# Score products of a retention layer issued in turn over four row groups, with a third group of batches in the scans' PSUM banks and a new set of planner figures

## The chip, the cores and the metric

The program runs on one core of a Trainium2 chip. The metric is the device time of one execution in microseconds; a kernel's time is the median over its runs. A trace exists of one execution, whose own time is given beside its span (from the first instruction to the last).

Names of the engines: PE is the matrix engine (TensorE; PEld is its weight loads), DVE is VectorE, ACT is ScalarE, POOL is GpSimd, SP is the engine that only issues transfers here. PEclk is the share of full speed that PE's clock was granted.

## The reference, cut to what matters

Two layers work on x of shape (16, 256, 128), that is 16 batches of 256 positions. Each layer is an attention-like part and an expert part, both with a modulated layer norm ahead and a gated residual behind. All is float32.

1. **Layer 0, retention.** Eight heads of 16 features keep a state that decays from position to position. The kernel computes it by products:

```python
S = g * S + k_t[..., :, None] * v_t[..., None, :]
y_t = jnp.einsum('bhde,bhd->bhe', S, q_t)
```

   Behind it come a group norm over the positions and a projection.

2. **Layer 0, experts.** Each of 8 experts chooses its 64 best positions of every batch (`top_k` over positions), with an exact Gelu between two products.
3. **Layer 1, selective scan.** For 256 inner features and 16 states each, with a short convolution and gates around it:

```python
dA = jnp.exp(dt_t[..., None] * A)
h = dA * h + dt_t[..., None] * b_t[:, None, :] * u_t[..., None]
y = jnp.einsum('bdn,bn->bd', h, c_t)
```

4. **Layer 1, experts.** Each position goes to its best 2 of 8 experts, with a gated product of width 448.

## The kernel before, in words

**A planner writes the order.** The function `adaln_two_layers` states the work as *chains*: a chain is a list of operations of which each follows the one before it, with an urgency (`pl.chain(urgency)`). A chain may need the end of other chains' steps (`need`, `done`) or a free buffer (`take`, `give`). `Plan.issue` then goes through all chains while the program is built. It keeps a clock for each engine, takes the operation that can start first (among those within 0.15 us on that engine, the one of the smallest urgency), and so fixes the order of every engine's instructions. Durations come from the table `USUAL` (by engine, name of the output and its length) or, where it has no entry, from the `us=` of the call. The urgencies are in `U`: `A` is that of the four groups of retention, `E` of the layer-0 experts with `Eh` and `Eo` for their two products, `front` of what prepares a batch for the scans, and `exp`, `dB`, `scan`, `sum` of the scans' parts. On the chip every engine then runs its list in order and waits where an operand is missing. In the trace nearly every operation has line 174, that of the planner's call, so rows are told apart by tiles.

**Retention** (`retention(g)`, groups of four batches, g = 0 to 3). For a batch b, `scores(b)` norms x, transposes it (pta, hTa), makes q and k together (pqk), copies q, and makes two masked copies of k, ke and ko, with the even and the odd heads (DVE and ACT). Then pv and v, pk, kd and the state S. The score products follow: for each j of four, the 32 features 32j to 32j+31 (two heads) of ke and ko are multiplied with q for both halves of the positions, four products of 32 rows x 128 x 128 into a bank of PSUM that is j's own. DVE multiplies the bank with the decay table and writes pr (`pr{b}_{j}`, 128 x 512). `outputs0(b)` multiplies pr with v into four groups of 32 columns (py) and takes statistics (yst). `group_norm`, `project` and `expert_scores` follow for a group, and `choose` selects the positions, in a series of small DVE operations (m, wk, sp).

**The banks.** The tuple `own` says where the score products go. The names va, vg, vx, vy are tokens for the four banks which the scans use later (two for dA, one for h, one for the sums ya). The token e stands for two banks of the common pool `ps_w`, shared with other work. `EARLY` is the number of groups that use the scans' banks; `recur`, which adds the scans' chains to the plan, waits for their last score products and for the first group's Gelus.

**Layer-0 experts** (`experts_of(q)`, four batches at a time): gather by products (gg, px, xin), first product (ph), Gelu (hg), second product (pye, ysb), and the way back by products (gt, pos, fres).

**Scans** (`scans`, 256 units: 16 batches of 16 units, a unit having 128 partitions and two scans of 256 positions side by side). `front(b)` makes bt, u and dd for a batch, with pb, pxs and pdt on PE; spl on ACT uses a logarithm. For each unit ACT makes dA by two exponentials into one of two PSUM buffers, POOL makes dB (twelve buffers), DVE runs the scan h, multiplies h with ct into dB, and PE sums (ya). The exponential, the logarithm and the exact Gelu need different function tables on ACT; the build adds a table load wherever the next function isn't in the table at hand. The planner isn't told of these loads but by durations: `us=1.88` for a Gelu of the last three expert groups (0.6 for the first) and 3.2 for the logarithm.

**Layer-1 experts** (`expert(g, j)`, 92 tiles of 128 positions; px, pa, pg, sl, pm, py at line 1576, yt) start while the scans run; 47 tiles come behind the last scan.

Of the kernel before, what the change touches and what calls it, by code (L numbers as in the profile page):

```python
# [11 lines left out]
F32 = mybir.dt.float32  # L12
# [3 lines left out]
ALU = mybir.AluOpType  # L16
# [3 lines left out]
P = 128  # L20
B, L, D = 16, 256, 128
NCH = L // P
H0, DH = 8, 16
E, CAP, HF = 8, 64, 512
# [3 lines left out]
T = 2 * L  # L28
# [1 line left out]

GROUPS = ((0, 1), (2, 3), (4, 5, 6), (7,))

U = dict(A=(-27.35, -16.05, -15.45, 46.6), setup=-34.65, E=(-42.15, 39.3, 75.0, 33.85), Eh=-43.75, Eo=-49.25,
         norm=34.2, front=-6.85, gates=-73.15, rep=-27.35, exp=-15.05, dB=91.6, ct=32.55, sum=6.05, scan=87.0,
         yg=38.9, back=-20.75, prep=-42.55, route=12.25, send=-52.55, tile=23.35, comb=38.9, wts=23.25,
         depth=2, gap=1.3, wlag=25, fw=27.7)

USUAL = {
    "S": {("A", 32): 0.189, ("xna", 128): 0.411, ("hTa", 256): 0.515, ("q", 256): 0.355, ("ko", 256): 0.444,
         ("v", 512): 0.557, ("yT", 256): 0.349, ("yn", 256): 0.521, ("xnf", 128): 0.408, ("hTf", 256): 0.529,  # L40
         ("p_tok", 64): 0.237, ("sp", 256): 0.331, ("xn", 128): 0.418, ("hTm", 256): 0.527, ("bt", 512): 0.55,
         ("thu", 512): 0.55, ("spy", 256): 0.444, ("dx", 256): 0.447, ("spy", 512): 0.598, ("thz", 512): 0.55,
         ("xnq", 128): 0.411, ("xin", 512): 0.734, ("dA", 255): 0.447, ("ct", 512): 0.55, ("om", 128): 0.373,
         ("sq", 128): 0.26, ("d", 8): 0.189, ("xT", 128): 0.332, ("sl", 448): 0.511, ("mT", 512): 0.551,
         ("yt", 128): 0.258, ("acc", 128): 0.376, ("d", 12): 0.189, ("d", 4): 0.189},
    "V": {("A", 32): 0.193, ("lnr", 128): 0.241, ("wdl", 128): 0.289, ("wdtp", 256): 0.386,
         ("wop", 256): 0.289, ("zp", 256): 0.289, ("wbc", 128): 0.209, ("xsp", 128): 0.193, ("sw", 128): 0.265,
         ("wcv", 512): 0.675, ("dg", 128): 0.241, ("rms", 1): 0.096, ("gater", 8): 0.193, ("seg", 32): 0.193,
         ("seg", 64): 0.193, ("seg", 96): 0.193, ("st_a", 6): 0.211, ("mv_a", 2): 0.099, ("ke", 256): 0.458,
         ("kd", 128): 0.271, ("S", 128): 0.277, ("pr", 512): 0.629, ("yst", 6): 0.404, ("gst", 2): 0.174,  # L50
         ("m", 4): 0.289, ("gm", 4): 0.145, ("dm", 4): 0.201, ("vv", 4): 0.145, ("res", 256): 0.41,
         ("st_g", 6): 0.199, ("mv_g", 2): 0.078, ("p_tok", 16): 0.169, ("gmx", 8): 0.209, ("p_tok", 64): 0.241,
         ("wk", 256): 0.371, ("m", 8): 0.273, ("sp", 256): 0.519, ("slot_tok", 64): 0.217, ("st_m", 6): 0.199,
         ("mv_m", 2): 0.075, ("u", 512): 0.656, ("spd", 512): 0.638, ("sz", 512): 0.651, ("gg", 512): 0.913,
         ("ysb", 512): 0.656, ("gt", 1024): 1.416, ("fres", 256): 0.397, ("h", 512): 1.185, ("dB", 512): 0.663,
         ("yg", 512): 0.651, ("st_o", 6): 0.211, ("mv_o", 2): 0.088, ("om", 512): 0.747, ("st_f", 6): 0.211,
         ("mv_f", 2): 0.088, ("hs", 128): 0.271, ("gbh", 256): 0.404, ("lgs", 32): 0.181, ("i", 8): 0.153,
         ("d", 8): 0.145, ("ws", 8): 0.145, ("wts", 8): 0.169, ("iF", 16): 0.145, ("oh", 64): 0.169,
         ("o", 64): 0.241, ("tot", 128): 0.289, ("t", 64): 0.337, ("inc", 64): 0.771, ("nt", 64): 0.675,
         ("nte", 8): 0.217, ("cum", 8): 0.337, ("et", 184): 0.337, ("ee", 23): 0.337, ("eis", 23): 0.193,  # L60
         ("base", 8): 0.156, ("row", 64): 0.241, ("pf", 16): 0.289, ("pos", 16): 0.145, ("sl", 448): 0.596,
         ("acc", 128): 0.361, ("d", 12): 0.675, ("ws", 12): 0.193, ("wts", 12): 0.193, ("iF", 24): 0.193,
         ("oh", 96): 0.193, ("o", 96): 0.289, ("tot", 192): 0.289, ("t", 96): 0.193, ("inc", 96): 0.386,
         ("nt", 96): 0.289, ("et", 248): 0.386, ("ee", 31): 0.386, ("eis", 31): 0.193, ("row", 96): 0.289,
         ("pf", 24): 0.386, ("pos", 24): 0.193, ("d", 4): 0.096, ("ws", 4): 0.193, ("wts", 4): 0.193,
         ("iF", 8): 0.289, ("oh", 32): 0.145, ("o", 32): 0.193, ("tot", 64): 0.193, ("t", 32): 0.193,
         ("inc", 32): 0.193, ("nt", 32): 0.193, ("et", 120): 0.289, ("ee", 15): 0.289, ("eis", 15): 0.193,
         ("row", 32): 0.193, ("pf", 8): 0.193, ("pos", 8): 0.193},
    "T": {("pwd", 128): 0.266, ("pwdt", 128): 0.31, ("pw", 128): 0.31, ("pwt", 128): 0.144,
         ("pta", 128): 0.219, ("pqk", 256): 0.576, ("pv", 256): 0.595, ("pk", 128): 0.354, ("sc", 128): 0.298,  # L70
         ("py", 128): 0.12, ("pgm", 4): 0.377, ("po", 128): 0.313, ("ptf", 128): 0.222, ("gs", 8): 0.291,
         ("pT", 128): 0.188, ("psl", 32): 0.144, ("ptn", 128): 0.259, ("pb", 256): 0.598, ("pxs", 256): 0.567,
         ("pdt", 256): 0.49, ("pz", 256): 0.482, ("px", 512): 1.061, ("ph", 256): 0.486, ("pye", 128): 0.127,
         ("pos", 128): 0.254, ("pc", 256): 0.618, ("ya", 256): 0.571, ("ya", 512): 0.302, ("pom", 128): 0.298,
         ("ph", 128): 0.141, ("pl", 8): 0.236, ("rank", 64): 0.288, ("px", 128): 0.245, ("pm", 128): 0.144,
         ("rank", 96): 0.31, ("rank", 32): 0.266},
    "G": {("wveo", 64): 0.198, ("ihx_a", 8): 0.198, ("iy_a", 8): 0.204, ("it_a", 8): 0.204, ("nb_a", 8): 0.26,
         ("qd", 128): 0.47, ("ihx_y", 4): 0.198, ("iy_y", 4): 0.198, ("it_y", 4): 0.226, ("gs", 4): 0.297,
         ("gbi", 4): 0.236, ("x", 256): 0.768, ("ihx_g", 8): 0.322, ("rs", 8): 0.217, ("it_g", 8): 0.212,
         ("nb", 8): 0.211, ("ihx_m", 8): 0.272, ("iy_m", 8): 0.217, ("it_m", 8): 0.206, ("nb_m", 8): 0.211,  # L80
         ("spd", 512): 1.312, ("dx", 512): 1.287, ("dB", 512): 1.263, ("ihx_o", 4): 0.297, ("iy_o", 4): 0.198,
         ("it_o", 4): 0.195, ("nb_o", 4): 0.211, ("ihx_f", 4): 0.198, ("iy_f", 4): 0.195, ("it_f", 4): 0.195,
         ("nb_f", 4): 0.223, ("ssq", 4): 0.223, ("ihx_r", 4): 0.186, ("iy_r", 4): 0.195, ("it_r", 4): 0.195,
         ("acc", 256): 0.727},
}
NG = len(GROUPS)
CGS = [len(ks) * T // P for ks in GROUPS]
# [56 lines left out]
class Plan:  # L144
# [84 lines left out]
    def need(self, *keys):  # L229
        self.pre += [("need", k) for k in keys]  # L230

    def take(self, name, n=1):
        self.pre.append(("take", name, n))
# [4 lines left out]
    def done(self, *keys):  # L238
        self.items[-1][5].extend(("done", k) for k in keys)

    def give(self, *names):
        self.items[-1][5].extend(("give", k) for k in names)
# [75 lines left out]
def adaln_two_layers(ctx: ExitStack, tc: tile.TileContext, a: dict, out: bass.AP):  # L318
# [33 lines left out]
    at = before.enter_context(tc.tile_pool(name="at", bufs=2))  # L352
# [17 lines left out]
    with tc.tile_pool(name="su", bufs=1) as su, tc.tile_pool(name="sups", bufs=2, space=PSUM) as sups:  # L370
# [3 lines left out]
        sc = fixed(su, [P, 2, B], "sc")  # L374
        nc.scalar.activation(sc.rearrange("p l b -> p (l b)"), pk0[:, PK0["c"][0] : PK0["c"][1]], AF.Silu)
        for l in range(2):
            pm = sups.tile([P, 4, B], F32, tag="pm", name=f"pm{l}")
# [10 lines left out]
            g = su.tile([B, 2, D], F32, tag="g", name=f"g{l}")  # L388
# [22 lines left out]
    slot_tok = fixed(r1, [P, NCH, B, E], "slot_tok")  # L411
# [6 lines left out]
    first = C1["tri"][0]  # L418
# [25 lines left out]
    pl = Plan(tc)  # L444
    V, S, G, T_, Q = pl.V, pl.S, pl.G, pl.T, pl.Q
    need, take, done, give = pl.need, pl.take, pl.done, pl.give
    NHC, NREP = 12, 3
    EARLY = 2
    TPX, TPO = "w", "w"
    NYT, NHT, NBT, NU, NGT = 4, 4, 2, 2, 3  # L450
    pl.tokens(hTa=2, an=8, xna=2, q=2, v=2, kd=1, pr0=1, pr1=1, pr2=1, pr3=1, yT=NYT, tabA=4, yn=1, res=1)
# [79 lines left out]
    def retention(g):  # L531
# [22 lines left out]
        base = 4 * g  # L554
# [31 lines left out]
        def scores(b):  # L586
# [56 lines left out]
            done(("S", b))  # L643


            for j in range(4):
                pl.chain(up + b / 100)
                need(("qk", b), *([("pr", b - 1, j)] if b > first else []))
                pool, tag, tok = own[j]
                psj = pool.tile([P, NCH, 2, P], F32, tag=tag, name=f"sc{b}_{j}")  # L650
                prj = prs[b, j] = at.tile([P, NCH, 2, P], F32, tag=f"pr{j}", name=f"pr{b}_{j}", bufs=1)
                r = slice(32 * j, 32 * j + 32)
                take(f"pr{j}")
                take(tok)
                for ch in range(NCH):
                    cs = slice(ch * P, (ch + 1) * P)
                    for par, kk in enumerate((ke, ko)):
                        T_.matmul(psj[:, ch, par, :], kk[r, cs], q[r, cs], start=True, stop=True, us=0.17)
                V.tensor_tensor(
                    prj.rearrange("p c q t -> p c (q t)"), psj.rearrange("p c q t -> p c (q t)"),  # L660
                    dec[:, j, :].unsqueeze(1).to_broadcast([P, NCH, 2 * P]), ALU.mult, us=0.69,
                )
                give(tok)
                done(("pr", b, j))

        def outputs0(b):
            g, i = b // 4, b % 4
# [1098 lines left out]
```

## Time and profile before

| | |
|---|---|
| runs of the kernel | 1371.86, 1361.18, 1370.16 us; median 1370.16 |
| profiled execution | 1377.36 us, span 1375.6 us |
| busy in the span | PE 1089.2 us (79%), DVE 958.5 (70%), ACT 793.5 (58%), POOL 760.9 (55%) |
| granted clock of PE, mean | 0.862 |
| first scan starts, last scan starts | 276.1 us, 1152.5 us |
| score products on PE | 512 records (two for each product), 23.1 to 416.5 us |
| table loads on ACT | 82 records, 105.2 us, 1283 ns each |

How to read it: "busy" counts the time in which at least one instruction of an engine runs. A matrix product in float32 leaves two records of PE and two of PEld, and they overlap, so the mean duration of a record isn't what it costs in a series. The idle time ahead of a group is put down to the engine that ended the wait.

### The profile page before, as it was taken

The page shows a single profiled execution, that of the slowest core. Times are in us where ns is not written, and L with a number is a line of the kernel's source. Part 1 is how long each engine was busy: PE and PEld are TensorE (multiplying, and loading weights), DVE is VectorE, ACT ScalarE, POOL GpSimd, SP SyncE. Part 2 cuts the span into 40 slices and gives each one's busy share as a digit, 9 for nine tenths or more (in the row PEclk, how much of TensorE's full clock was granted, in tenths as well). Part 3 has the DMA queues.
Part 4 walks back from the last instruction along what each step waited for, and adds up shares of the span by engine and source line. Part 5 has one row for each costly group of instructions (what it writes and reads, how often), then busy time and mean ns, then how long its engine had stood idle before and what let it go on. Part 6 is the DMA issues. An engine that isn't in the chain of part 4 may idle for free.

```text
span 1375.6 us, 20606 instructions
## 1 busy us (share of the span) xinstructions
PE 1089.2 (79%) x6227; PEld 740.2 (54%) x6227; DVE 958.5 (70%) x1860; ACT 793.5 (58%) x1665; POOL 760.9 (55%) x1241
## 2 busy tenths in 40 slices
PE   6988998988897777956687877787776787779983
PEld 4765875656564454633455545444444454456652
DVE  4556156477979878888977888999886896353332
ACT  2333343588555888546697664677666464534442
POOL 3220121564457766678567876867768764740164
PEclk9977997989977898776788897899789799999997
DMA  5152322255444555655367631544353342221122
GB/s 141 44 162 79 123 78 56 66 167 143 125 139 113 155 150 146 164 180 143 99 180 195 150 107 52 142 133 130 88 148 100 92 126 67 72 58 40 47 80 56
DMA packets 118396, 156.05 MB, mean 113 GB/s; under 512 B 17880, under 2 KB 88608, under 8 KB 117920
## 3 DMA queue, kind: packets, MB, share of 16 engines
q1 hardware_dynamic: 113040, 138.84, 37.0%
q0 software_dynamic: 4256, 9.18, 2.3%
q10 hardware_dynamic: 992, 6.71, 1.6%
q8 instruction: 53, 0.87, 0.3%
q14 instruction: 55, 0.45, 0.1%
HBM read 127.64 MB, written 27.04 MB: 112 GB/s over the span
## 4 chain that ended last, share of the span: by engine, by line
PE 37%; DVE 26%; POOL 15%; ACT 10%; issue 8%; DMA 3%; DVEq 0%; another core or an unknown queue 0%; POOLq 0%; SPq 0%; ACTq 0%
DVE h L174 10%; PE sc L174 4%; DVE dB L174 4%; PE py L1576 4%; PE pye L174 3%; PE pa L1546 3%; ACT L174 3%; POOL dB L174 2%; PE pg L1546 2%; ACT dA L174 2%; PE ph L174 2%; PE ya L174 2%; PE py L174 2%; POOL got L174 2%; PE px L174 2%
## 5 line engine op out<-in xcount | busy, mean ns | idle before, releaser
L174 POOL TENSOR_TENSOR dB<-rep,bt 128x512 f32<-128x512 f32 x256 | 326.0, 1295 | 161.3 <-DMA rep<-dd 77.9
L174 DVE TENSOR_TENSOR_SCAN h<-dA,dB 128x512 f32<-128x512 f32 x256 | 314.6, 1229 | 72.0 <-ACT dA L174 37.2
L174 ACT ACTIVATE dA<-rep,A 128x255 f32<-128x255 f32 x512 | 241.0, 475 | 145.3 <-DVE h L174 133.4
L174 DVE TENSOR_TENSOR dB<-h,ct 128x512 f32<-128x512 f32 x256 | 175.9, 687 | 6.1
L1576 PE MATMUL py<-w,mT 112*128 x736 | 113.1, 302 | 46.9 <-ACT mT L174 39.6
L1576 PEld LDWEIGHTS py<-w,mT 112*128 112x128 f32 x736 | 101.4, 209 | 79.5 <-ACT mT L174 52.8
L174 POOL DMA_INDIRECT got<-ydr,pos x64 | 61.6, 962 | 108.4 <-ACT mT L174 67.6
L174 DVE SCALAR_TENSOR_TENSOR sl<-sl,pa 128x448 f32<-128x448 f32 x92 | 56.6, 615 | 86.1 <-ACT sl L174 76.4
L174 PE MATMUL ya<-dB,c 128*32 128x512 f32 x512 | 88.9, 687 | 30.4 <-DVE dB L174 30.4
L174 ACT ACT_TABLE_LOAD x82 | 105.2, 1283 | 1.5
L1546 PE MATMUL pa<-w,xT 128*128 x184 | 97.8, 616 | 9.7 <-ACT yt L174 2.5
L1546 PE MATMUL pg<-w,xT 128*128 x184 | 92.2, 585 | 6.9 <-DVE sz L174 3.3
L174 ACT COPY mT<-pm 112x512 f32<-112x512 f32 x92 | 53.5, 582 | 52.1 <-PE pm L174 38.8
L1494 POOL DMA_INDIRECT disp<-hs,pos x64 | 64.0, 1001 | 34.4 <-DVE pos L174 21.1
L174 PE MATMUL ph<-xin,fw 128*128 128x256 f32 x256 | 71.5, 422 | 12.3 <-ACT hg L174 6.3
L174 PE MATMUL pye<-fw,hg 128*64 128x128 f32 x1024 | 72.2, 306 | 5.1 <-ACT hg L174 5.1
L174 PEld LDWEIGHTS pye<-fw,hg 128*64 128x64 f32 x1024 | 67.1, 158 | 16.6 <-ACT hg L174 6.3
L174 PE MATMUL pxs<-hTm,wcv 128*128 128x256 f32 x256 | 70.9, 423 | 0.0
L174 PE MATMUL pm<-c,sl 128*112 128x128 f32 x368 | 60.5, 289 | 12.1 <-DVE sl L174 10.9
L174 ACT ACTIVATE yt<-py 128x128 f32<-128x128 f32 x92 | 25.1, 273 | 77.2 <-PE py L1576 59.0
L174 PEld LDWEIGHTS ph<-xin,fw 128*128 128x128 f32 x256 | 50.1, 206 | 30.7 <-ACT hg L174 9.4
L174 DVE TENSOR_TENSOR sl<-sl,pg 128x448 f32<-128x448 f32 x92 | 57.1, 621 | 10.1 <-DVE sl L174 0.9
(295 smaller groups left out, 2264.3 us busy)
## 6 DMA issues: line engine op xcount, KB each, us to landing
rep<-dd SPq DMA_DIRECT2D x128, 512.0 KB
fw<-in_fw SPq DMA_DIRECT2D x64, 256.0 KB
gt<-spd SPq DMA_DIRECT2D x64, 128.0 KB
pr<-spd SPq DMA_DIRECT2D x64, 128.0 KB
dd<-dx SPq DMA_DIRECT2D x16, 512.0 KB
xt<-disp SPq DMA_DIRECT2D x92, 64.0 KB
ydr<-yt SPq DMA_DIRECT2D x92, 64.0 KB
w<-in_w ACTq DMA_DIRECT2D x3, 1792.0 KB
```

What stands on the lines that cost most here:

```text
L174: return plan.op(key, us, lambda: getattr(real, name)(*args, **kw), lag)
L1494: i = nc.gpsimd.indirect_dma_start(out=disp[g], out_offset=bass.IndirectOffsetOnAxis(ap=pos[g][:, c, r, :], axis=0), in_=hss[GROUPS[g][c / ...
L1546: nc.tensor.matmul(o, xT, w[:, bass.ds(which[0], 1), :].rearrange("p o i -> p (o i)"), start=True, stop=True)
L1576: nc.tensor.matmul(py, mT[:, ic, :], w2[:, bass.ds(which[0], 1), ic, :].rearrange("p o d -> p (o d)"), start=(ic == 0), stop=(ic == NFC - 1),)
```

## The change

Three things change together.

1. In `scores`, the loop over j is turned inside out: the products of several j are issued in turn, instead of four for one j after four for another. Groups g < `EARLY` go round all four j; later ones go round two and then the other two, and take both tokens e at once. The four DVE products (`pr`) follow behind the last score product of their set.
2. `EARLY` goes from 2 to 3: twelve batches use the scans' banks, and the scans' chains are added to the plan only behind batch 11's score products.
3. All urgencies in `U` and most durations in `USUAL` have new values. `Plan` itself is not changed, so what the new figures were fitted to shows only in the order that comes out of them.

```diff
-U = dict(A=(-27.35, -16.05, -15.45, 46.6), setup=-34.65, E=(-42.15, 39.3, 75.0, 33.85), Eh=-43.75, Eo=-49.25,
-         norm=34.2, front=-6.85, gates=-73.15, rep=-27.35, exp=-15.05, dB=91.6, ct=32.55, sum=6.05, scan=87.0,
-         yg=38.9, back=-20.75, prep=-42.55, route=12.25, send=-52.55, tile=23.35, comb=38.9, wts=23.25,
-         depth=2, gap=1.3, wlag=25, fw=27.7)
+U = dict(A=(-27.45, -14.7, 24.25, 39.05), setup=-69.45, E=(-10.7, 57.55, 9.1, 41.85), Eh=-31.75, Eo=-63.75,
+         norm=-2.5, front=-65.85, gates=-61.55, rep=-69.25, exp=-70.35, dB=59.4, ct=66.35, sum=30.9,
+         scan=51.45, yg=-30.35, back=33.45, prep=-35.25, route=-69.45, send=47.05, tile=49.95, comb=53.0,
+         wts=34.25, depth=2, gap=1.3, wlag=25, fw=-8.1)
...
-    "T": {("pwd", 128): 0.266, ("pwdt", 128): 0.31, ("pw", 128): 0.31, ("pwt", 128): 0.144,
-         ("pta", 128): 0.219, ("pqk", 256): 0.576, ("pv", 256): 0.595, ("pk", 128): 0.354, ("sc", 128): 0.298,
...
+    "T": {("pwd", 128): 0.266, ("pwdt", 128): 0.184, ("pw", 128): 0.31, ("pwt", 128): 0.316,
+         ("pta", 128): 0.22, ("pqk", 256): 0.641, ("pv", 256): 0.576, ("pk", 128): 0.361, ("sc", 128): 0.11,
...
-    EARLY = 2
+    EARLY = 3
...
-            for j in range(4):
+            side_by_side = ((0, 1, 2, 3),) if g < EARLY else ((0, 1), (2, 3))
+            for js in side_by_side:
                 pl.chain(up + b / 100)
-                need(("qk", b), *([("pr", b - 1, j)] if b > first else []))
-                pool, tag, tok = own[j]
-                psj = pool.tile([P, NCH, 2, P], F32, tag=tag, name=f"sc{b}_{j}")
-                prj = prs[b, j] = at.tile([P, NCH, 2, P], F32, tag=f"pr{j}", name=f"pr{b}_{j}", bufs=1)
-                r = slice(32 * j, 32 * j + 32)
-                take(f"pr{j}")
-                take(tok)
+                need(("qk", b), *(("pr", b - 1, j) for j in js if b > first))
+                pss = {}
+                for j in js:
+                    take(f"pr{j}")
+                if g < EARLY:
+                    for j in js:
+                        take(own[j][2])
+                else:
+                    take("e", len(js))
+                for j in js:
+                    pool, tag, _ = own[j]
+                    pss[j] = pool.tile([P, NCH, 2, P], F32, tag=tag, name=f"sc{b}_{j}")
+                    prs[b, j] = at.tile([P, NCH, 2, P], F32, tag=f"pr{j}", name=f"pr{b}_{j}", bufs=1)
                 for ch in range(NCH):
                     cs = slice(ch * P, (ch + 1) * P)
                     for par, kk in enumerate((ke, ko)):
-                        T_.matmul(psj[:, ch, par, :], kk[r, cs], q[r, cs], start=True, stop=True, us=0.17)
-                V.tensor_tensor(
-                    prj.rearrange("p c q t -> p c (q t)"), psj.rearrange("p c q t -> p c (q t)"),
-                    dec[:, j, :].unsqueeze(1).to_broadcast([P, NCH, 2 * P]), ALU.mult, us=0.69,
-                )
-                give(tok)
-                done(("pr", b, j))
+                        for j in js:
+                            r = slice(32 * j, 32 * j + 32)
+                            T_.matmul(pss[j][:, ch, par, :], kk[r, cs], q[r, cs], start=True, stop=True, us=0.35 / len(js))
+                for j in js:
+                    V.tensor_tensor(
+                        prs[b, j].rearrange("p c q t -> p c (q t)"), pss[j].rearrange("p c q t -> p c (q t)"),
+                        dec[:, j, :].unsqueeze(1).to_broadcast([P, NCH, 2 * P]), ALU.mult, us=0.69,
+                    )
+                    give(own[j][2])
+                    done(("pr", b, j))
```

## The prediction

> **What bounds the kernel now.** I read the busy time by stage first, cut where the first scan starts (275 us) and where the last one ends (1155 us).
>
> ```profile
> core 0: us, PE busy (x) PEld busy (x) DVE busy (x) ACT busy (x) POOL busy (x), PEclk, DMA share, GB/s
> 72.00:115.00 43.00, 33.60 (x177) 24.79 (x178) 29.67 (x119) 14.23 (x32) 8.96 (x37) 0.67 0.52 143
> 115.00:275.00 160.00, 152.24 (x1093) 113.55 (x1091) 73.57 (x203) 67.83 (x131) 38.65 (x108) 0.88 0.28 83
> 275.00:1155.00 880.00, 678.68 (x3619) 441.19 (x3618) 742.30 (x1235) 593.88 (x1214) 607.75 (x878) 0.84 0.49 133
> 1155.00:1376.00 221.00, 166.55 (x885) 116.59 (x884) 79.38 (x184) 94.28 (x239) 85.03 (x134) 0.93 0.21 59
> ```
>
> Ahead of the scans PE is the limit (152 of 160 us in the second row; 9.4 us idle in the first). While the scans run, DVE is the fullest engine. Behind them the last expert tiles run. The rows of tile h say how tightly DVE is bound in the middle:
>
> ```profile
> L174 DVE TENSOR_TENSOR_SCAN h<-dA,dB x256: 1194/1231/1232, 276.1 to 1152.5; 128x512 f32<-128x512 f32 x128
> L174 DVE TENSOR_TENSOR dB<-h,ct x256: 646/692/693, 277.3 to 1154.9; 128x512 f32<-128x512 f32 x128
> its engine sat idle before it (us, times) until:
>   ACT dA L174: 37.2, 21
>   POOL dB L174: 13.7, 8
> ```
>
> A scan and its product take 1.23 + 0.69 us; where nothing lies between, scans start 2.09 us apart. From the first start to the last are 876 us: 255 × 2.09 = 533, some 300 of other DVE work between the scans, and some 43 in which DVE stands. So in this stage a microsecond of other work taken off DVE is worth nearly a microsecond, and one taken off PE is worth nothing by itself.
>
> **The change, part by part.**
>
> *1. Score products in turn over four row groups.* The chain of waits shows both forms of small product:
>
> ```profile
> 25.25 2.20 PE sc L174 x26
> 28.50 1.57 PE py L174 x34
> 405.04 2.00 PE sc L174 x8
> ```
>
> A product leaves two records. The third line is one row group alone at half clock: 8 records, 2.0 us less some 0.2 of drain, 0.22 each, hence 0.111 at full clock. Products of one group follow one another at that step. py goes round four column groups, and its 16 products with one full-size product take 1.57 us: four in one step. In the first line the groups overlap only where one ends and the next begins. If row groups overlap as column groups do, a batch's 16 products become 8 steps: 0.9 + 0.2 = 1.1 us, against 2.2 in one piece.
>
> The old order often cuts them up. I counted, in the orders of PE's instructions in the two programs, the unbroken stretches of score products and, in each, the steps of the group with most work. Before: 69 stretches, 456 steps; after: 38 and 186. A step costs 0.111 / 0.86 = 0.129 us at the mean clock (0.862), a stretch some 0.2 us of drain: 456 × 0.129 + 69 × 0.2 = 73 us before. The trace agrees: from start to start, with overlaps counted once, the 256 products hold PE for 74 us (0.29 each). After: 186 × 0.129 + 38 × 0.2 = 32 us. PE gains some 42 us.
>
> It costs something too: the four banks fill together, so DVE's first mask product starts about 0.5 us later, and py waits for the fourth: 1.1 + 4 × 0.69 = 3.9 us after the scores start, 3.25 before (25.18 to 28.43 us). PE's queue has pqk, pv, pta and a pk in between (some 2.3 us), so 0.3 to 0.5 us per batch show: 4 us over the first batches, nothing later, where other work lies between.
>
> *2. Twelve batches in the scans' banks, and the new urgencies.* Scans are admitted only when batch 11's mask products are done. The order goes further: all 16 batches' scores (12.7 before) stand ahead of the first scan on PE. The first exponentials on ACT stand behind pdt of the second batch in both orders. PE's work up to there, other instructions at their mean start-to-start time, is 192.5 us plus 203 score products at 0.29 (59), 251 us; it really ended at 269.5. After: 230.0 us (py, pv, pqk, pk of further batches, and six more ph and a pye of the second expert group) plus 32 = 262. That is +10. The third group's retention now stands where PE idled 9.4 us waiting for the first selection: −7. With the 4 us of part 1 the first scan starts **about 6 us later** (−8 to +30; the low end if the idle time fills wholly, the 4 us hide and the other terms are 5 us smaller, the high end if row groups overlap half as well, 186 × 0.129 = 24 us more).
>
> DVE takes its share of that retention before the first scan too: 12 mask products (12 × 0.69 = 8.2), one group's whole selection (11.4 us busy in the trace, 202 to 216 us), 2 ke, 3 kd, 3 S, 4 yst with their aggregates (5.0) and a group norm's small operations (1.1). Sum: **26 us that leave the scans' queue**. They go where DVE was busy 74 of 160 us, beside PE. If that cover were missing they would come back as a later first scan, which the high end holds.
>
> *3. What the plan puts into ACT's queue.* No arithmetic is added anywhere, but the table loads rise from 83 to 118. ACT's order shows why: the three later expert groups' Gelus stood in pairs (24 visits among the exponentials); now 40 visits, 38 of them with one Gelu. What a visit does to the scans:
>
> ```profile
> 286.58 1.23 DVE L174 TENSOR_TENSOR_SCAN h<-dA,dB 128x512 f32<-128x512 f32 x1 [0.29 <-POOL dB L174]
> 286.91 1.28 ACT L174 ACT_TABLE_LOAD   x1
> 288.20 1.08 ACT L174 ACTIVATE hg<-ph 128x512 f32<-128x512 f32 x2
> 289.31 1.28 ACT L174 ACT_TABLE_LOAD   x1
> 290.60 1.38 ACT L174 ACTIVATE dA<-rep,A 128x255 f32<-128x255 f32 x3
> 291.17 1.23 DVE L174 TENSOR_TENSOR_SCAN h<-dA,dB 128x512 f32<-128x512 f32 x1 [2.62 <-ACT dA L174]
> ```
>
> dA has two buffers, so ACT is less than a scan ahead; this pair held it for 3.7 us and the scan came 2.6 us late. Behind dA wait the scan, its product, and everything in DVE's queue. Over the 24 visits, the stretches like this one sum to 30 us, 1.26 each: others fell where DVE had work of its own. A single Gelu makes the visit 0.6 us shorter; taking 0.6 from each stall I find leaves some 0.9. So 38 × 0.9 + 2 × 1.26 = 37, **+7**. Bounds: −7 (short visits fit under the 2.09 us period and cost half) to +50 (no cover: 40 × 2.0 = 80). I take +4, nearer the low end, since spread visits let ACT catch up.
>
> Here a rule speaks against the change. The Trainium skill (ScalarE: Activation LUTs, What ACT_TABLE_LOAD costs) gives a switch 1283 ns and about 1380 ns of drain, 2.66 us in all, and its section on table sets asks to batch calls by set. By that, 35 more loads are 93 us of ACT. In the rows above 1.29 us lie between the start of a load and of the activation behind it (286.91 to 288.20, 289.31 to 290.60); no second drain shows. By the row they are 45 us. ACT was busy 594 of 880 us; with 45 more and some 15 moved ahead it stands near 625 of 860, 73%: tight, not the bound. By the rule with the 75 old loads of the stage counted likewise, it would be near 775 of 860, 90%, and the scans would often wait for ACT. The trace decides.
>
> *4. The rest.* The tail's instructions are the same on PE (47 tiles behind the last scan in both) and nearly in the same sequence: 0 ± 5. The queues of SP and POOL keep their counts; per batch POOL's work stays below DVE's but once, with twelve buffers of lead. A dd and its rep loads go in the same alternation with the weights; I cost this at nothing, and if a rep came late POOL's dB would show it (77.9 us of such waits now, mostly hidden by the lead).
>
> **Sum.** +6 − 26 + 4 + 0 = −16 us. The profiled execution took 1377.4 us (span 1375.6), so 1361; the median of the runs shown is 7 us lower, 1370.2, so **1354 us** there.
>
> **The rivals** (on the median).
>
> *Exchange, not gain.* The 26 us come off the scans and go back before them: the row groups overlap half as well, the first scan comes 30 us late, and with +4 on ACT the sum is +8: 1378. For it: PE is the limit there, and 16 batches' scores instead of 12.7 must pass. Against it: py's measured step. If the groups did not overlap at all (the change not doing what it says), part 1 would give back its 42 us: 1396.
>
> *The table loads decide; slower.* Place: ACT between exponentials in the first nine batches. Price: 2.0 us for each of 40 visits without cover, +50 over now; with +6 − 26 that is +30: 1400. It decides from a mean stall near 1.25 us (no gain left: 40 × 1.25 = 30 + 20) and costs 1% from 1.6. For it: 28 of the 40 visits have less than 1 us of DVE work beside them in the order (16 of 24 before). Against it: the trace's uncovered visits range from 0.5 to 3.4 us, many being partly absorbed.
>
> *More than counted.* The start is 8 us earlier and ACT gains 7: −41, 1329. For it: the idle 9.4 us and the clock of 0.67 there. Against it: the selection's serial chain stays.
>
> **How the numbers follow.** Forecast (its own range 1338 to 1368) 0.5; exchange 0.22, with no overlap counted in it; table loads 0.18; more 0.1. A change of about 1% can be told from none. The forecast is below 1356.5 in some 0.42 of its 0.5 chances, with the fourth case 0.52; the exchange, the rest of the forecast and the milder table stalls lie within 1% (0.28); most of the table case and no overlap lie above 1384 (0.20). Leaving out 1 in 10 on each side, the range is 1326 to 1392.
>
> **What would show each step.** Score products: PE's rows for sc near 32 us start to start, 16 in about 1.1 us. First h at 276 ± 10 becomes 282. First to last h: 854 instead of 876, with other DVE work between the scans near 275. Waits of h for dA near 37 us; if above 65 the second rival is right. From the last h to the end 223 us. The forecast is wrong if the first scan starts after 296, or if the stage keeps its 876 us.

## The result, and the profile after

The changed kernel takes 1377.14 us (median of 20 runs, 1368.45 to 1392.73) where the kernel before takes 1368.85 on the same chip (20 runs): a ratio of 1.0061, with the 95 % interval 1.0034 to 1.0088. It is 0.6 % slower; the forecast was 1354.

The products themselves did what they were meant to do. The chain of work that ended last has, for the first batches (start us, us, what; x32 is the 16 products of a batch, two records each):

```profile
24.06 0.87 PE sc L175 x22
29.58 1.10 PE sc L175 x32
35.62 1.10 PE sc L175 x32
```

A batch's products take 1.10 us. Before, they came in pieces, of which 26 of the 32 records alone took 2.20; run e3 below has all 32 in sequence, in 2.75 us (TensorE's granted clock is 1.00 from 25 to 50 us in both). Counted from start to start, the 256 products hold TensorE for 33.3 us, and took 74.1 before (32 was forecast).

The next view is of the tile h, cut to the scans' own row and their waits; the times after the colon are the shortest, middle and longest in ns, then first and last start:

```profile
L175 DVE TENSOR_TENSOR_SCAN h<-dA,dB x256: 1196/1231/1232, 313.5 to 1162.5; 128x512 f32<-128x512 f32 x128
its engine sat idle before it (us, times) until:
  ACT dA L175: 29.1, 22
  POOL dB L175: 15.3, 7
```

First and last start, read against 276.1 and 1152.5 before, split the time into three stages:

| stage (us) | before | forecast | after |
|---|---|---|---|
| to the first scan | 276.1 | 282 | 313.5 |
| first scan to last scan | 876.4 | 854 | 849.0 |
| last scan to the last write's start | 219.6 | 223 | 209.5 |

The scan stage gave 27 us, 5 more than forecast. The front took 37, of which 6 were forecast. The 10 us of the tail are not the change's: two runs below (e5 and e6), which have the two kernels' orders, have tails of 209.2 and 207.7, so it is the profiled run of before that had 10 us extra there. (No table load falls into the tail. One order's tail can differ by 10 us between executions: e3, with the changed kernel's order there, has 219.4.) The run's own time was also 8.5 us above its median. Without them, +37 and -27 are the whole difference, about +10 against the measured +8.

The windows show how the front was spent (busy us and number of instructions of PE, PEld, DVE, ACT, POOL; then TensorE's clock and the DMA's share and rate):

```profile
115.00:275.00 160.00, 135.07 (x1038) 98.64 (x1036) 88.55 (x262) 58.47 (x121) 27.02 (x84) 0.84 0.22 69
275.00:1155.00 880.00, 657.44 (x3422) 420.18 (x3420) 712.71 (x1161) 636.69 (x1231) 601.93 (x869) 0.85 0.50 134
```

From 115 to 275 us TensorE was busy for 152.2 us of 160 before, and is for 135.1 now: it waits more. VectorE does 15 us more there (88.6 for 73.6) and 30 us less in the scan window (712.7 for 742.3). ScalarE does 43 us more in the scan window (636.7 for 593.9), and the costliest groups tell what:

```profile
L175 ACT ACT_TABLE_LOAD x117 | 150.1, 1283 | 2.0
```

There were 82 loads in 105.2 us. The last figure is ScalarE's idle time before them, 2.0 us for all 117.

**Where the front loses time.** In both orders the first scan follows pdt of the second batch, which starts at 268.3 us before and at 306.7 after. The first two rows are TensorE up to there, before and after (us, busy us and instructions, clock, DMA share and rate). The other two are its waits for kd up to that point, before and after (us in all, times, longest); kd is VectorE's product from which each batch's state S is made.

```profile
0.00:268.30 268.30, 237.32 (x1669) 0.87 0.31 91
0.00:306.70 306.70, 251.65 (x2075) 0.87 0.29 84
PE pk L174 <- DVE kd L174: 7.9, 2, 4.6
PE pk L175 <- DVE kd L175: 18.3, 5, 9.2
```

So of 38.4 us, 14.3 are more work of TensorE, and 24.1 are more waiting (55.1 for 31.0). Waits for kd are 10 of the 24. The longest shows what stands behind them:

```profile
258.18 1.23 PE L175 MATMUL pk<-v,kd 128*128 128x128 f32 x4 [9.23 <-DVE kd L175]
```

From 245.1 to 257.9 us VectorE's queue has, ahead of this kd, the whole selection of the third group, which the new order moved ahead of the scans (its copy into wk came at 366.9 before, and comes at 245.1 now). Another 6.6 us of the waiting lie before 103 us; the rest is scattered.

**Group 0's selection** also comes late. It starts with a copy of pT into wk. Its transposes come at 102.8 us before and 103.2 after, but the copy follows at 103.4 before, and at 127.9 after. The timeline of VectorE between them, cut to what carries it (start us, us, what, in brackets the idle time before and its releaser):

```profile
105.01 0.68 DVE L175 TENSOR_TENSOR pr<-sc,c 128x512 f32<-128x512 f32 x1
...
105.68 1.87 DVE L175 TENSOR_TENSOR pr<-sc,c 128x512 f32<-128x512 f32 x3
...
112.66 0.42 DVE L175 TENSOR_TENSOR res<-po,tabA 128x256 f32<-128x256 f32 x1 [1.76 <-PE po L175]
...
118.74 0.42 DVE L175 TENSOR_TENSOR res<-po,tabA 128x256 f32<-128x256 f32 x1 [1.04 <-PE po L175]
119.08 1.28 DVE L175 TENSOR_TENSOR pr<-sc,c 128x512 f32<-128x512 f32 x2
120.27 1.63 DVE L175 BATCH_NORM_STATS2 st_g<-x 128x6 f32<-128x128 f32 x8
...
122.37 1.25 DVE L175 TENSOR_TENSOR pr<-sc,c 128x512 f32<-128x512 f32 x2
...
127.94 0.41 DVE L175 COPY wk<-pT 32x256 f32<-32x256 f32 x1 [3.73 <-PE py L175]
```

Two buffers decide this. In the code, the copy takes pr3, in which wk lies, and all four parts of the buffer tabA. Group 1's projection (res) needs a table in tabA. In the changed order that table's transfer is issued at 94.1 us, ahead of the selection (130.7 before, behind it), so the copy can be planned only when the fourth res has given tabA back, at 119.2. By then the next batch's block, which takes pr0 to pr3 in one step, holds pr3, and the copy waits for its py until 127.9. So some 16 us stand at tabA and 9 at pr3. Taking the four pr together isn't enough for the delay: e1, e2, e8 and e9 do it too, have tabA's transfer behind the copy, and copy 0.8 to 7.4 us after pT. In e3, e4, e6 and e7 it is ahead of the copy, which comes 24 to 30 us after pT.

This delay carries over to group 0's px (117.6 to 147.3), but TensorE had other batches' retention meanwhile: from 103 to 148 us it stood idle for 10.4 us, 5.7 before. What the late selection alone costs the first scan isn't shown.

### The profile page after: what moved, and what is told of

It is laid out like the page before. It is cut to its first block, busy times and chain, and to the rows that moved or that the text cites. A ratio compares the mean times of both kernels' runs of the same rounds, so it can differ in the third digit from the quotient of the medians.

```text
span 1375.5 us, 20601 instructions
## 1 busy us (share of the span) xinstructions
PE 1054.0 (77%) x6227; PEld 703.2 (51%) x6227; DVE 953.6 (69%) x1860; ACT 839.1 (61%) x1700; POOL 760.5 (55%) x1241
## 3 DMA queue, kind: packets, MB, share of 16 engines
q1 hardware_dynamic: 113040, 138.84, 37.4%
## 4 chain that ended last, share of the span: by engine, by line
PE 31%; DVE 27%; ACT 16%; POOL 12%; issue 7%; DMA 6%; DVEq 0%; POOLq 0%; SPq 0%; ACTq 0%
DVE h L175 9%; ACT L175 5%; DVE dB L175 4%; ACT dA L175 4%; PE py L1588 3%; PE ya L175 3%; PE pye L175 2%; PE py L175 2%; PE pa L1558 2%; PE pxs L175 2%; DMA rep<-dd 2%; PE pg L1558 2%; POOL got L175 2%; DVE sl L175 2%; PE ph L175 2%
## 5 line engine op out<-in xcount | busy, mean ns | idle before, releaser
L175 DVE TENSOR_TENSOR_SCAN h<-dA,dB 128x512 f32<-128x512 f32 x256 | 314.6, 1229 | 65.2 <-ACT dA L175 29.1
L1588 PE MATMUL py<-w,mT 112*128 x736 | 107.5, 292 | 30.9 <-ACT mT L175 24.3
L1588 PEld LDWEIGHTS py<-w,mT 112*128 112x128 f32 x736 | 97.2, 201 | 59.4 <-ACT mT L175 35.5
L175 PE MATMUL ya<-dB,c 128*32 128x512 f32 x512 | 95.5, 710 | 35.7 <-DVE dB L175 35.7
L175 PE MATMUL ph<-xin,fw 128*128 128x256 f32 x256 | 76.3, 434 | 19.6 <-ACT hg L175 10.3
L175 PE MATMUL pxs<-hTm,wcv 128*128 128x256 f32 x256 | 76.1, 448 | 0.0
L175 POOL TENSOR_TENSOR qd<-q,c 128x128 f32<-128x128 f32 x16 | 7.9, 493 | 117.1 <-ACT q L175 117.0
```

The lines of the kernel that those rows point to most:

```text
L175: return plan.op(key, us, lambda: getattr(real, name)(*args, **kw), lag)
L1588: nc.tensor.matmul(py, mT[:, ic, :], w2[:, bass.ds(which[0], 1), ic, :].rearrange("p o d -> p (o d)"), start=(ic == 0), stop=(ic == NFC - 1),)
```

## The experiments

Theory A was that the late selection of group 0 makes the kernel slow; theory B that interleaving or TensorE's clock does; theory C and D that the loads do. Each kernel's ratio is to the kernel before on its own chip. Where the planner's input is edited, it plans everything again with the weights it has. For every kernel the table has the three stages of its profiled run, in us.

| kernel | ratio, interval | to first scan | scans | tail |
|---|---|---|---|---|
| e1, batches 8-11 held | 1.0354, 1.0303-1.0405 | 277.3 | 923.8 | 228.7 |
| e2, interleaving alone | 1.0151, 1.0105-1.0197 | 263.7 | 902.6 | 230.0 |
| e3, products in sequence | 1.0260, 1.0216-1.0303 | 349.4 | 840.1 | 219.4 |
| e4, Gelu chains in pairs | 1.0409, 1.0358-1.0460 | 324.0 | 861.0 | 253.6 |
| e5, before, Tanh for Gelu | 0.9879, 0.9841-0.9917 | 279.7 | 860.4 | 209.2 |
| e6, after, Tanh for Gelu | 0.9869, 0.9826-0.9911 | 310.7 | 820.0 | 207.7 |
| e7, EARLY = 2 | 1.0524, 1.0478-1.0570 | 314.0 | 876.2 | 243.0 |
| e8, loads in the plan | 0.9852, 0.9824-0.9880 | 273.1 | 850.4 | 211.5 |
| e9, the same, other weights | 0.9655, 0.9627-0.9683 | 276.1 | 840.4 | 197.9 |

### e1: hold the third group back

```diff
-            need(("an", g))
+            need(("an", g), *([("slot", 0)] if b >= 8 else []))
```

> The changed kernel with one demand more: the retention of batches 8 to 11 may be planned only after group 0's experts are selected. Theory A (the first scan is late because VectorE reaches group 0's selection, the copy of pT into wk, behind mask products and projections of the later batches): wk of group 0 comes back from 127.9 us to near 104, the first px from 147 to near 118, the first scan from 313.5 to 265-285, and the scan stage, which gets the four batches' VectorE work back (about 4 x 4 mask products and what belongs to them), grows from 849 to about 865; 1345-1360 us in all. Theory B (TensorE itself is slower in the front, at a clock of 0.84 instead of 0.88 and with four row groups side by side): wk may come back, but the first scan stays at 300 or later, and the time at 1370 or more. Theory C (activation tables): 118 loads or so remain, so the time stays within 5 us of 1377.

The front came out as theory A has it. The tile wk of this kernel:

```profile
L175 DVE COPY wk<-pT x4: 395/412/414, 102.9 to 597.5; 32x256 f32<-32x256 f32 x4
```

Its first copy is at 102.9 us, and the first scan at 277.3, 36 us earlier than in the changed kernel. But the demand does more than bring the copy back: ahead of the second batch's pdt TensorE has 210.2 us of work instead of 251.7, and waits no less (58.1 us; 55.1). So e1 doesn't show that the late copy makes the first scan late. That scan also stands alone: the second starts at 312.0 (315.6 in the changed kernel), behind mask products and the third group's selection.

The whole is 40 us slower than the changed kernel. The scan stage has grown by 75 us, most of it in two gaps: the 34.7 us up to the second scan, and 53.8 between the last scan of batch 3 and the first of batch 4, whose experts are late (from the second group's first ph to its first pos 126 us; 113 in the changed kernel, 71 before). So **an early first scan is not by itself an early end**. Theory A's numbers for the front held; its forecast of the whole was missed by 57 us or more (by the ratio 1417 us, against at most 1360).

### e2: the interleaved loop alone, in the old plan's terms

```diff
-            for j in range(4):
+            side_by_side = ((0, 1, 2, 3),) if g < EARLY else ((0, 1), (2, 3))
+            for js in side_by_side:
...
```

> The kernel before with only the new loop over the score products (four side by side for the first two groups, two by two for the others); the planner's weights, durations and EARLY = 2 are those of before. Theory A: the products take about as little of TensorE as in the changed kernel (33 us from start to start for the twelve interleaved by four; the pairs in between), the selection of group 0 stays where it was (wk near 104), so the first scan is not later than the 276 of before: 255-275; the scan stage stays within 10 us of 876, and the whole comes out at 1350-1365 us. Theory B (interleaving itself holds TensorE up): first scan after 280 and 1370 or more. Theory C (tables): about as many loads as before (83), so nothing is lost or won by them.

The first scan comes 12 us earlier, as expected and against theory B. The scans take 26 us longer: VectorE's empty time between first and last scan grows from 136.5 to 167.0 us, most of all at batches 7 and 8. The whole is 1.5 % slower, where theory A had it faster.

### e3: the products in sequence, all orders else kept

```diff
-                for ch in range(NCH):
-                    cs = slice(ch * P, (ch + 1) * P)
-                    for par, kk in enumerate((ke, ko)):
-                        for j in js:
-                            r = slice(32 * j, 32 * j + 32)
+                for j in js:
+                    r = slice(32 * j, 32 * j + 32)
+                    for ch in range(NCH):
+                        cs = slice(ch * P, (ch + 1) * P)
+                        for par, kk in enumerate((ke, ko)):
```

> The changed kernel, plan and order of everything else alike, but inside a block the score products run row group after row group again. Theory A: the score products take about 74 us from start to start for 256 as before, 2.3 us for a block of 16 instead of 1.1; the front waits on VectorE for most of this time, so the first scan moves from 313 by 0 to +20, and the time is 1380-1395 us. Theory B (the interleaved form is what slows the front): the first scan gets earlier than 310 and the time less than 1375. In any case the spacing of the first four batches' yst grows from 6.0 to near 8.6.

Here every other order stays, so it is the clean measure of the interleaving: 1.0260 against 1.0061 is 2.0 %, some 27 us (18 to 37 by the ends of the intervals). A block takes 2.75 us, and all 256 products 62.3 from start to start (2.3 and 74 expected), 29 more than in the changed kernel. The first scan moves from 313.5 to 349.4, more than expected (0 to +20): ahead of the second pdt TensorE has 39 us more work and waits 5 less. So the front is still TensorE's for the most part. (The clock was lower as well, 0.81 from 115 to 275 us for 0.84; part of the 39 is that.) That interleaving holds the front up, theory B, is excluded. In the changed plan the interleaving earns 27 us, and something else spends more than that.

### e4: the Gelu chains less urgent

```diff
-            pl.chain(-30)
+            pl.chain(-80)
```

> The changed kernel with the Gelu chains of the experts' hidden layer less urgent (-80 instead of -30), so that they come in pairs again: 76 table loads instead of 118, the front as in the changed kernel. Theory A: the first scan stays at 310-316, 54 us of ScalarE work go (42 loads of 1.29), but ScalarE has slack between the scans; the time moves by less than 6 us, 1371-1380. Theory C (tables decide): the time falls by 15-40 us, to 1340-1362, with the scan stage down from 849 to 825 or less.

42 loads fewer in the program, and 3.5 % slower than the changed kernel. The tail alone has 44 us more. As a test of the loads it fails, since it also changes when each expert runs; it says only that pairs bought in this way cost more than they give.

### e5 and e6: the loads without a new plan

```diff
-                S.activation(..., banks[e, hp][0], AF.Gelu, us=1.88 if q else 0.6)
+                S.activation(..., banks[e, hp][0], AF.Tanh, us=1.88 if q else 0.6)
```

> The kernel before with the experts' Gelu replaced by Tanh, which shares its table with the other activations: the output is another, every instruction of every other engine and its order are the same, and ScalarE's program has 49 table loads fewer (34 instead of 83). Theory D (the loads that the new plan scatters are what took its gain): ScalarE loses 49 x 1.29 = 63 us of loads, of which about a third lay on the path: 15-25 us, 0.982-0.989 of before. Theory A (only the front's queue made the change slow; loads cost nothing because ScalarE has slack): within 6 us of before, 0.996-1.002.

> The changed kernel with the same replacement (the output is another; all orders stay): 84 table loads fewer (34 instead of 118). Theory D: 84 x 1.29 = 108 us of loads go, 40-50 us of them on the path: 0.970-0.978 of before, which is 15-25 us less than the kernel before with the same replacement, so the new plan is better than the old one where loads are alike. Theory A: still about 0.6 % behind its twin, within 6 us of the changed kernel, with the first scan still 30 us later than the twin's.

These two compute something else, but all orders stay, Tanh takes as long as Gelu (0.59 us for 0.60), and both programs now have 34 loads. With the loads alike, the two orders are equally fast (0.9879 and 0.9869, intervals overlapping almost wholly). Before gains 1.2 %, 16.5 us for 49 loads: 0.34 us for each. After gains 0.9869 / 1.0061, 1.9 % or 26 us for 84: 0.31 us for each. Each load is 1.283 us long, so about a quarter of it reaches the end. The higher clock of these runs isn't the reason: at like clocks (0.868 to 0.873) e5 takes 1351 to 1355 us and before 1364 to 1367, e6 1348 to 1358 and the changed kernel 1369 to 1378. The wait that they cause is seen at the scans; e6's h:

```profile
its engine sat idle before it (us, times) until:
  POOL dB L175: 17.8, 8
  ACT dA L175: 3.9, 5
```

In the changed kernel h waited for dA 29.1 us. VectorE's empty time between first and last scan falls by 29 us (135.9 to 106.6), in before's order by 16 (136.5 to 120.7). Between the first scan and the last, the new order gains 40 us on the old one where loads are alike (820.0 for 860.4) and 27 where they are not. So the 35 loads that it adds cost about 11 us by the ratios (35 x 0.32), whose intervals leave some 9 us to either side; by the scan stage of the traces, 13. That is the sign of the result: without them the change would come out about even. It is not what theory D had on record: e6 was to be 15 to 25 us ahead of its twin, and is not ahead measurably. The late first scan (310.7 for 279.7) still takes the rest. Theory A alone, by which loads cost nothing, is refuted too.

### e7: only two groups in the scans' banks

```diff
-    EARLY = 3
+    EARLY = 2
```

> The changed kernel with EARLY = 2: only the first two groups' products are interleaved by four in the scans' banks, the third and fourth by two in the ordinary banks, and the plan is made again with the changed kernel's weights and durations. Theory E (the weights fit this one plan, and any other list of demands makes them a poor plan): the front stays late (first scan 300-315), the third and fourth selections come later, and the whole is 30-60 us slower than the changed kernel, 1.03-1.05 of before. Theory F (it is the third group in the scans' banks that costs): first scan before 300, and faster than before, 0.98-1.00.

Theory E held for the front: the first scan doesn't move (314.0), and the fourth group's selection ends at 690 us instead of 542. The whole lies just above its range (1.0524; 1.03 to 1.05). Theory F is refuted. The run doesn't show what the third bank group is worth in a plan made for two.

### e8 and e9: a plan that knows the loads

```diff
+TABLE = {AF.Gelu: 1, AF.Exp: 2, AF.Tanh: 2, AF.Ln: 3}
...
+            if h.table and h.table != loaded:
+                us, loaded = us + 1.29, h.table
...
-                S.activation(..., AF.Gelu, us=1.88 if q else 0.6)
+                S.activation(..., AF.Gelu, us=0.6)
-        S.activation(lg, y, AF.Ln, bias=one1, us=3.2)
+        S.activation(lg, y, AF.Ln, bias=one1, us=0.722)
-            pl.chain(-30)
+            pl.chain(-348.42)
```

The weights U are new as well, searched by the planner's own sum with this term. The last line is that of e9.

> The changed kernel's code for the products, and a plan that is made again with one term more: each activation whose function needs another table than the one before it on ScalarE is charged 1.29 us (Gelu and Ln lose their flat surcharges, 1.88 to 0.6 and 3.2 to 0.722), and the weights were searched anew by the planner's sum with this term. Its order has 79 loads instead of 118, group 0's selection stands behind 4 projection products and 8 statistics again instead of 8 and 16, and the first scan follows 238 us of TensorE's work instead of 262. Theory G (the change was slow because its weights were chosen without the loads and with group 0's selection behind group 1's projection; both can be mended with the interleaving kept): first scan at 270-285, scan stage 800-830, whole 1320-1345 us, 0.965-0.985 of before. Theory B' (the gain of the interleaving is spent whatever the plan, because VectorE's work between the scans only moves): 1360-1380, 0.995-1.01.

> As e8_loads_in_plan, with the weights of another end of the same search, whose planned sum is 1 us longer: it tells how much of the result is the luck of one plan. Theory G: within 12 us of e8, 0.965-0.99 of before, first scan at 270-285. If plans with about equal sums scatter by more than 20 us on the chip, the sum is no guide.

Both beat both kernels: e8 takes 1348.50 us and e9 1322.02, where before takes 1368.80. e9 is 3.5 % faster than before, and by the two ratios 4.0 % faster than the changed kernel. The group of the loads, the scans' row and the front's window of e9:

```profile
L175 ACT ACT_TABLE_LOAD x79 | 101.4, 1283 | 1.4
```

```profile
L175 DVE TENSOR_TENSOR_SCAN h<-dA,dB x256: 1191/1231/1232, 276.1 to 1116.4; 128x512 f32<-128x512 f32 x128
```

```profile
115.00:275.00 160.00, 141.77 (x1039) 104.30 (x1031) 70.07 (x205) 68.17 (x134) 37.44 (x106) 0.87 0.27 82
```

The first scan is where it was before the change, to the tenth of a us, and the selection is back (slot_tok, its end, at 114.3; 116.1 before, 141.2 after). Ahead of the second pdt TensorE has 222.7 us of work and 48.7 of waiting. VectorE again does 70 us of work from 115 to 275 us, so this plan doesn't take work out of the scan stage: VectorE is busy there for 737.7 us, as before (739.9), where the changed kernel has 713.2. What fell is its empty time between first and last scan: 136.5 us before, 135.9 after, 102.6 in e9. Some 11 us more come from e9's tail, which has the last products of 47 tiles instead of 50. Theory G holds for e9's whole; e8 lies just outside (0.9852 and 1348.5; 0.985 and 1345 were the ends), and the scan stage of both misses its range (850 and 840 against 800 to 830). The two plans differ by 1 us in the planner's sum and by 26 us on the chip, over the 20 that were set as the mark: the sum tells a good plan from a bad one, not one good plan from another. How much of the gain is the loads' term and how much the new search isn't separated.

The runs also tell which part of the change makes the first scan late. The interleaving with the old weights has it at 263.7 (e2), the changed weights with `EARLY` = 2 at 314.0 (e7), and interleaving and third group with other weights at 273 and 276 (e8, e9). So it is the order that comes from the changed weights. (e8 and e9 keep the changed durations but for Gelu and Ln, and also have the loads' term.)

## Why the prediction was wrong, by its own steps

- **Step 1, the products.** Right in size: 33.3 us for 256 products (32 forecast), 1.10 us for a batch's. The "2.2 in one piece" was a misreading: that line has 26 of a batch's 32 records, and a whole batch in sequence takes 2.75 (e3). e3 prices the interleaving at 27 us in this plan.
- **Step 2, the first scan: the step that failed.** "About 6 us later" (−8 to +30) was forecast, and 37.4 came. Its sum was +10 for TensorE's work ahead of the second pdt, −7 for an idle stretch that the third group's retention would fill, and +4 for later mask products. The work rose by 14.3. The waiting, 3 us less by the forecast, rose by 24.1: that term failed, and holds 27 of the 31 us missed. It was taken that TensorE, 95 % busy there, would stay so, and that VectorE's 26 us of moved work would be covered. They were not wholly: TensorE waited 10 us more for kd, of which 9.2 at once behind the third group's selection, one of the pieces moved. The other 14 us of waiting are scattered, and their cause stays open. The prediction named the missing cover and left it to the high end of its range (+30), which 37.4 exceeds; "wrong if the first scan starts after 296" was the right mark. It looked at neither pr3 nor tabA, by which group 0's selection moved.
- **The scans.** -27.4 us for -22 forecast. VectorE's busy time in the stage fell by 26.7 us (26 forecast), and its empty time stayed (136.5 and 135.9).
- **Step 3, the loads.** Their number was right (118 in the program, 117 in the trace); their price was +4 for 35 more, and e5 and e6 make it about 11. ScalarE was busy 72 % of the scan window (636.7 of 880), as the row with 1.29 us a load had it (73 %), not 90 %. The wait of h for dA was forecast at 37 and fell to 29.1, which hides it: without the Gelu loads it is 3.9. The rival "table loads decide" at 1400 was about four times too dear, and yet the loads are what separates slower from even, within the intervals.
- **Step 4, the tail.** Right: two runs show 208 and 209 for the two orders. The profiled run of before was a poor base here, by 10 us.
- **The rival "exchange, not gain"** (1378, the first scan 30 us late) came nearest to the number, by luck: it had the row groups overlapping half as well, and they overlap as forecast. What was exchanged is VectorE's work: it left the scans, and part of it came back as TensorE's waiting ahead of them.

## What to carry to other kernels

To forecast a milestone, count two terms of the engine that reaches it: its work, and its waiting for instructions of other engines, each behind whatever the new order puts ahead of it. An engine that is 95 % busy before a change can stand still a sixth of the time after it, and work that moves "beside" it can hold it up. Look also at every buffer that two tiles share, for it decides which may go first. Then see the whole: changing one piece of a plan and keeping weights that were chosen for another (e1, e2, e4, e7) lost time each time, while a plan made for all costs at once, table loads among them, kept the interleaving's gain. To price something that sits between engines, replace it without touching any order (e3, e5, e6); these were the runs that could be read.

## What was not expected of the hardware

- A table load holds ScalarE for 1.283 us, and costs 0.31 to 0.34 us of the whole, about alike in two different orders, though ScalarE is only 61 % busy on the mean (839 of 1375 us): here even an engine with that much slack passed a quarter on.
- TensorE's granted clock in the front of the changed kernel is not higher for less work: 0.84 from 115 to 275 us with 135 us busy, where 0.88 stood with 152. But the busy time of the stretch doesn't tell the clock: e1 has 0.89 there with the same 135 us, and e6, in the changed kernel's order, 0.85 with 133.
